# Four convolution layers in one kernel: where the next image's products are asked for, and how layer 3 is entered

## The chip, the cores and the metric

One NeuronCore of a Trainium2 chip runs the whole network in a single launch. The metric is the device time of that launch in microseconds, from the first to the last instruction. Five engines work side by side, each with its own instruction stream: TensorE (PE; its weight loads are shown as PEld), VectorE (DVE), ScalarE (ACT), GpSimd (POOL) and SyncE (SP), which here issues nearly all DMA transfers.

## The reference

The input has 4 images of 256 channels and 48 x 48 pixels. Four layers follow each other, each as `x = x + layer(group_norm(x))`, in float32:

```python
# layer 0: 49 attention weights a pixel, from a 7x7 convolution with dilation 2
k = relu(conv(x, w1, 7x7, dilation 2) + b1)            # 128 channels
k = relu(batch_norm(conv(k, w2, 1x1) + b2))            # 49 channels
attn = softmax(k, axis=1)
out = sum over the 49 taps p of: shifted(x, p) * attn[:, p]
# layer 1: 3x3 convolution of the signs of x with the signs of the weights
# layer 2: 3x3 convolution with ternary weights and a scale for each output channel
# layer 3: linear attention over windows of three sizes
q, k = sigmoid(Wq x), sigmoid(Wk x);  v = Wv x, normalised for each head
for each window: attn = (q . sum over the window of k v) / (q . sum over the window of k)
out = Wout concat(the three) + bout
```

The group norm needs the mean and variance of whole groups of channels over an image. So each layer of an image begins with a chain of small steps (statistics, a matmul that averages over groups, a reciprocal root), and nothing of that layer can start ahead of it.

## The kernel before

Layers 0 to 2 run image by image; layer 3 follows for all images. While image b is in its attention of layer 0, in layer 1 and in layer 2, the 7x7 convolution of image b + 1 is the filler: a generator whose products are asked for in small chunks where TensorE would otherwise wait. A call of `fill(us)` asks for about that much of it.

```python
def fill(us):
    next(side, None)
    owed += us
    while owed > 0:
        n = next(filler, None)          # the next chunk: up to three products of 0.52 nominal us each
        if n is None: owed = 0.0; return
        owed -= n
```

`conv0(b, extra)` is that convolution, in a form with fewer products: for seven points, one after the other, VectorE makes combinations of rows (`v`) and columns (`vx`) of the padded image, TensorE multiplies them by prepared weights (`cv<-vx,wt`), and VectorE gathers the outcome in `y` and `k`. It is 260 products an image. A point's own preparation is spread over the chunks of an earlier point: 8 operations with point 0, 18 each with points 2 and 4, 4 each with points 1, 3 and 5.

```python
class Stats:
    def end(self, wait):
        ... bn_aggr ...
        wait(1.5)                       # a chunk of the filler
        pe.matmul(ps, gmat, mv[:, :, 0]) ; ... ; dve.tensor_add(v, v, mv[:, :, 1])
        wait(2.5)
        pe.matmul(ps, gmat, v) ; ... rsqrt ...

def transpose_x(pad, k):
    for h in range(NPH // 2):
        tr = ps_tr.tile(...)            # one buffer
        ... four transpositions on TensorE ...
        act.copy(xT[...], tr)
        fill(0.7)

def attend(b):                          # layer 0 of image b, from k1 on
    for k in range(NBLK):               # NBLK = 5
        lg = logits(k1, k)              # lg<-w_sb,k
        e = softmax_begin(lg, k)
        ...
        if k < 2: xTs[k] = transpose_x(pad, k); fill(2.6)
        else: fill(4)
    ...                                 # fill(10), then apply0 for each block
```

Layer 2 works on an image in three thirds of 16 rows. For each third, `normalised(h)` normalises the rows, `combine(ts, at)` makes for each of four combinations of rows a high part (VectorE, then a cast on ScalarE) and a low part (a subtraction on GpSimd); TensorE then makes four tiles (`at`) for each of two output halves (`mo`), and `give` adds each to x on VectorE.

```python
def layer2(b, stats):
    m, r = stats.end(fill)
    ...
    ts = normalised(0)
    for at in range(N2):
        combine(ts, at)
        fill(2 if at == 0 else 1)
    for h in range(thirds):
        if b == B - 1 and h == 0:
            proj["first"][0].enough = True
        for mo in range(NCT):
            for at in range(N2):
                if b == B - 1: fill(1.2)
                ps = ps_cv.tile(...)    # two buffers
                ... 12 matmuls: cv<-v,wl ...
                if late: late()         # give of the tile before
                late = functools.partial(give, ps, h, mo, at)
                if mo == NCT - 1 and h < thirds - 1:
                    if at == 0: ts = normalised(h + 1)
                    combine(ts, at)
    if b + 2 < B: fetch_x(b + 2, 0)
    fill(2)
    late()
    m3, r3 = stats.end(fill)            # for layer 3
```

`prelude(b)` is the start of image b: its statistics, the padded copy, the first rows and columns of its convolution. It runs between layer 2 of image b - 2 and the attention of image b - 1, and uses up what is left of the filler.

```python
def prelude(b):
    ...; fill(7)
    for ct in range(NCT):
        for s in range(NRB): stats.take(xts[b], ct, s)     # 6 each
        fill(2)
    m, r = stats.end(fill)
    ... pad ...
    fill(3)
    while stage < len(POINTS) - 1: fill(1)
    for _ in rows_at(pad, (0.0, None)): fill(0.9)
    for _ in columns_at(0.0, XPOINTS[:2]): fill(1)
    fill_all()
    for _ in columns_at(0.0, XPOINTS[2:]): pass

for b in range(B):
    filler = conv0(b + 1, {}) if b + 1 < B else project_first()   # and here, for the last image: the masks
    stats = attend(b)
    ...
    layer2(b, layer1(b, stats))
    if b + 2 < B: prelude(b + 2)
    else: fill_all()
```

For the last image the filler is `project_first`: the projections (q, k, v) of image 0 for layer 3, in twelve groups. When layer 2 of the last image begins, the groups whose rows are not yet asked for are given up (`enough`) and are made inside layer 3. Layer 3 (`s<-qs,ks`, masked copies `sm`, then `acc<-sm,vs`) begins when q, k and v of its first block have been written and read back.

Of the kernel before, what the change touches and what calls it, by code (L numbers as in the profile page):

```python
# [13 lines left out]
BF16 = mybir.dt.bfloat16  # L14
# [7 lines left out]
P = 128  # L22
# [42 lines left out]
N2 = 4  # L65
# [80 lines left out]
def conv_preact_kernel(  # L146
# [101 lines left out]
    def start(job):  # L248
        active.append([step + 1, job])
# [37 lines left out]
    class Projection:  # L287


        def __init__(self, b, scr, psum, tag, shape):  # L290
            self.b, self.scr = b, scr
            self.psum, self.tag, self.shape = psum, tag, shape
            self.xn, self.uses, self.vs = {}, {}, {}

            self.enough, self.left = False, []

        def ps_tile(self):
            t = self.psum.tile(self.shape, F32, tag=self.tag, name="proj_ps")
            return t if len(self.shape) == 2 else t[:, 0]
# [1 line left out]
        def load(self, g, a, n):  # L301

            b = self.b
            yield from take("xr")
            if self.enough:
                free["xr"] += 1
                self.left.append(g)
                return
            xr = self.scr.tile([P, NCT, RB, W], F32, tag="xr", name="xr")
            sync.dma_start(  # L310
                out=xr,
                in_=x3_d[b][:, a * RB : (a + 1) * RB, :].rearrange(
                    "(ct p) r w -> p ct r w", p=P
                ),
            )
            yield FETCH
            yield from take("xn")
            xn = self.scr.tile([P, NCT, NKC, P], F32, tag="xn", name="xn")
            for ct in range(NCT):
                dve.tensor_scalar(  # L320
                    xn[:, ct].rearrange("p c (r x) -> p c r x", x=KC),
                    xr[:, ct].rearrange("p r (c x) -> p c r x", x=KC),
                    st3[:, b, 0, ct : ct + 1],
                    st3[:, b, 1, ct : ct + 1],
                    ALU.subtract,
                    ALU.mult,
                )
                yield 1
            free["xr"] += 1
            self.xn[g], self.uses[g] = xn, n  # L330
# [7 lines left out]
        def qk(self, g, a, name, mo):  # L338
            b = self.b
            while g not in self.xn:  # L340
                if g in self.left:
                    return
                yield 1
            yield from take("kt")
            yield from bank(1)
            ps = self.ps_tile()[:, 0:NB]
            for ct in range(NCT):
                pe.matmul(
                    ps,
                    proj[name][:, ct, mo * P : (mo + 1) * P],  # L350
                    self.xn[g][:, ct],
                    start=(ct == 0),
                    stop=(ct == NCT - 1),
                )
            self.used(g)
            yield 1
            t = self.scr.tile([P, NB], F32, tag="sg", name="sg")
            rows = t.rearrange("p (r c x) -> p c r x", c=NKC, x=KC)
            act.activation(
                rows, ps.rearrange("p (c r x) -> p c r x", c=NKC, x=KC), AF.Sigmoid  # L360
            )
            chans, cols = slice(mo * P, (mo + 1) * P), slice(a * NB, (a + 1) * NB)
            if name == "k":
                kt = self.scr.tile([P, NB], F32, tag="kt", name="kt")
                act.copy(kt.rearrange("p (c r x) -> p c r x", c=NKC, x=KC), rows)
            yield 1
            if name == "k":
                sync.dma_start(out=k_d[b][chans, cols], in_=kt)
            sync.dma_start(out=(q_d if name == "q" else kf_d)[b][chans, cols], in_=t)
            free["kt"] += 1  # L370
            made.add((name, b, mo, a))

        def v(self, g, a, c):
            b = self.b
            while g not in self.xn or (c > 0 and g not in self.vs):
                if g in self.left:
                    return
                yield 1
            if c == 0:
                yield from take("vt")  # L380
# [72 lines left out]
    with (  # L453
# [563 lines left out]
        def transpose_x(pad, k):  # L1017
# [4 lines left out]
            for h in range(NPH // 2):  # L1022
# [6 lines left out]
                            ident,  # L1029
                        )  # L1030
                act.copy(xT[:q, 2 * h : 2 * h + 2, :], tr)
                fill(0.7)
            return xT

        def apply0(xt, k, rows_at_hand, load_next, xTs):
# [46 lines left out]
        def attend(b):  # L1082

            k1, pad, xt = k1s.pop(b), pads[b], xts[b]
            begun = None
            xTs = {}
            for k in range(NBLK):
                lg = logits(k1, k)
                e = softmax_begin(lg, k)
# [54 lines left out]

        def layer1(b, stats):
            xt = xts[b]
            m, _ = stats.end(fill)
            neg = small.tile([P, NCT], F32, tag="neg", name="neg")
            dve.tensor_scalar_mul(neg, m, -1.0)
# [45 lines left out]
        def layer2(b, stats):  # L1195
# [68 lines left out]
                fill(2 if at == 0 else 1)  # L1264
            late = None
            for h in range(thirds):
                if b == B - 1 and h == 0:
                    proj["first"][0].enough = True
                for mo in range(NCT):
                    for at in range(N2):  # L1270
                        if b == B - 1:
                            fill(1.2)
                        ps = ps_cv.tile([P, R2, W], F32, tag="cv3", name="cv3")
                        n = 0
                        for ct in range(NCT):
# [11 lines left out]
                            late()  # L1287
                        late = functools.partial(give, ps, h, mo, at)

                        if mo == NCT - 1 and h < thirds - 1:  # L1290
                            if at == 0:
                                ts = normalised(h + 1)
                            combine(ts, at)
            if b + 2 < B:
                fetch_x(b + 2, 0)
            fill(2)
            late()
            m3, r3 = stats.end(fill)
            dve.tensor_copy(st3[:, b, 0, :], m3)
            dve.tensor_copy(st3[:, b, 1, :], r3)  # L1300

        def prelude(b):
# [6 lines left out]
            for ct in range(NCT):  # L1309
                for s in range(NRB):  # L1310
                    stats.take(xts[b], ct, s)
                fill(2)
            m, r = stats.end(fill)
            off0 = small.tile([P, 1], F32, tag="off0", name="off0")
            dve.scalar_tensor_tensor(off0, m[:, 1:2], -1.0, r[:, 1:2], ALU.mult, ALU.mult)
# [84 lines left out]
        with (  # L1400
# [13 lines left out]
            def project_first():  # L1414
# [7 lines left out]
                    sync.dma_start(out=proj[name], in_=src.rearrange("(ct p) o -> p ct o", p=P))  # L1422
                groups = [(a, ("k0", "v", "q0")) for a in range(NRB)]
                groups += [(a, ("k1", "q1")) for a in range(NRB)]
                proj["first"] = Projection(0, scr, ps, "ps", [P, 512]), groups
                start(paced(proj["first"][0].groups(groups), 1))
                while active:
                    advance()
                    yield 1.2
# [1 line left out]
            for b in range(B):  # L1431
                if b + 1 < B:
                    filler = conv0(b + 1, {})
                else:
                    ending.close()
                    wts3 = ctx.enter_context(tc.tile_pool(name="wts_qkv", bufs=1, side="right"))
                    filler = project_first()
                    masks = wts3.tile([P, NMASK], BF16, name="masks")
                    nc.gpsimd.dma_start(out=masks, in_=masks_in[:, 0:NMASK])
                stats = attend(b)  # L1440
                for _ in side:
                    fill(1)
# [11 lines left out]
    with (  # L1454
# [11 lines left out]
        nc.scalar.dma_start(out=wout_sb, in_=wout.rearrange("(kt p) o -> p kt o", p=P))  # L1466
        bout_sb = wts.tile([P, NCT], F32, name="bout_sb")
        nc.scalar.dma_start(out=bout_sb, in_=bout.rearrange("(ct p) -> p ct", p=P))
        mask = [
            masks[:, MASK_AT[i] : MASK_AT[i] + MROWS[i] * MCOLS[i]].rearrange(  # L1470
                "p (r c) -> p r c", c=MCOLS[i]
# [411 lines left out]
        order = [(b, ct, rb) for b in range(B) for ct in range(NCT) for rb in range(NRB)]  # L1883
        bank_m = ps_m, "st", [P, 512]


        made_first, groups = proj["first"]
        left = [groups[g] for g in made_first.left]
        if left:
            start(paced(Projection(0, scr, *bank_m).groups(left), 1))  # L1890
        for mo in range(NCT):
            start(in_turn([k_sums(b, a, mo) for b in range(B) for a in range(NRB)]))
        start(in_turn(norms(b, rb) for b in range(B) for rb in range(NRB)))

        seen_first = HALVES[0] // RB + 1
        until(("q", 0, 0, 0), *((what, 0, *at) for a in range(seen_first) for what, at in (("k", (0, a)), ("v", (a,)))))
        qs = {0: load_q(*order[0])}
        for a in range(seen_first):
            load_kv(0, 0, a)


        LOADS = {2: (0,), 3: (1, 2), 4: (3, 4), 5: (5,)}
# [120 lines left out]
```

## Time and profile before

The median of three runs is 3850.24 us (3838.81 to 3850.6). The profiled execution has a span of 3848.8 us and a mean granted TensorE clock of 0.943.

| stretch, us from the start | what runs there | PE busy, us | DVE busy, us | PE clock |
|---|---|---|---|---|
| 0 to 254.4 | image 0 and 1 begin, weights of layer 0 are prepared | 144.4 | 209.9 | |
| 254.4 to 455.5 | attention of image 0, weights of layers 1 and 2 | 152.2 | 91.8 | 0.80 |
| 455.5 to 563.2 | layers 1 and 2, image 0 | 101.2 | 68.5 | |
| 752.1 to 863.2 | layers 1 and 2, image 1 | 103.5 | 71.3 | |
| 863.2 to 945.5 | passage from image 1 to 2 | 68.6 | 68.2 | 0.95 |
| 945.5 to 1059.3 | attention of image 2 | 100.7 | 62.4 | 0.93 |
| 1059.3 to 1167.4 | layers 1 and 2, image 2 | 101.1 | 69.7 | |
| 1167.4 to 1237.0 | passage to image 3 | 65.5 | 41.8 | 1.00 |
| 1354.1 to 1480.0 | layers 1 and 2, image 3 | 110.4 | 76.6 | |
| 1480.0 to 1495.0 | entry to layer 3 | 4.4 | 6.7 | 0.59 |
| 1495.0 to 3848.8 | layer 3 | 2093.0 | 1543.0 | 0.97 |

A busy time close to the stretch's length says that the engine sets the pace there. The rest of the stretch is idle time, and the list of waits says what ended it. The granted clock is a share of full speed: at a lower one the same matmul takes longer, and that counts as busy. All operations go through one helper that keeps them in program order, so nearly every line of the profile has the same line number, and the groups are told apart by their tiles.

### The profile page before, as it was taken

What the parts mean: (1) busy time and instruction counts of PE and PEld (TensorE: products, weight loads), DVE (VectorE), ACT (ScalarE), POOL (GpSimd) and SP (SyncE); (2) the same over time, 40 slices, a digit from 0 to 9 for tenths busy, and PEclk for the clock granted to TensorE, in tenths of its full rate; (3) what the DMA queues carried; (4) which work ended last, traced back from release to release, by engine and by line L of the source; (5) the groups of instructions that cost most, each with busy time, mean ns of one, the idle gap of its engine ahead of it and who ended that gap; (6) DMA issues with size and microseconds to landing.
All of it is one profiled execution on the core that took longest, in us unless ns stands there. A gap on an engine that the chain in (4) does not pass through costs nothing. (4 is left out here: it accounts for less than half of the span.)

```text
span 3848.8 us, 68938 instructions
## 1 busy us (share of the span) xinstructions
PE 3300.0 (86%) x26534; PEld 1903.3 (49%) x26534; DVE 2483.7 (65%) x5119; ACT 1028.5 (27%) x2019; POOL 1511.4 (39%) x2183
## 2 busy tenths in 40 slices
PE   3678798998899788898789888899899899988998
PEld 2456676776777655443334333344444344443443
DVE  7873477567565356777656577765577856656655
ACT  0012111211110332443222333332243322233321
POOL 0000030020020023678764576765356856344432
PEclk9788799999999798999899999999999999999999
DMA  7734323413413332345443353434222434101122
GB/s 246 238 117 136 103 85 96 130 65 116 142 45 118 110 105 93 110 144 166 122 135 106 92 152 107 151 100 126 77 95 92 151 107 133 49 30 42 51 58 59
DMA packets 373018, 423.03 MB, mean 110 GB/s; under 512 B 129075, under 2 KB 328531, under 8 KB 371539
## 3 DMA queue, kind: packets, MB, share of 16 engines
q1 hardware_dynamic: 371491, 416.32, 35.0%
q8 instruction: 211, 3.46, 0.4%
q0 software_dynamic: 144, 1.52, 0.2%
q14 instruction: 116, 0.95, 0.1%
q10 hardware_dynamic: 1056, 0.79, 0.1%
HBM read 288.79 MB, written 131.25 MB: 109 GB/s over the span
## 5 line engine op out<-in xcount | busy, mean ns | idle before, releaser
L142 DVE TENSOR_TENSOR sm<-s,masks 128x112 f32<-128x112 f32 (+10 forms) x2592 | 1135.1, 492 | 785.0 <-PE s L142 329.9
L142 POOL TENSOR_TENSOR sm<-sm,masks 128x432 f32<-128x432 f32 (+14 forms) x1152 | 853.5, 754 | 956.9 <-ACT sm L142 705.1
L142 PE MATMUL s<-qs,ks 32*128 32x320 f32 (+3 forms) x5760 | 835.2, 503 | 197.6 <-DVE sm L142 147.3
L142 ACT COPY sm<-s 128x528 f32<-128x528 f32 (+2 forms) x1152 | 594.1, 534 | 1483.4 <-PE s L142 1195.6
L142 PE MATMUL acc<-sm,vs 128*32 128x384 f32 (+18 forms) x13440 | 879.2, 385 | 14.9 <-POOL sm L142 14.6
L142 PEld LDWEIGHTS s<-qs,ks 32*128 32x128 f32 x5760 | 375.6, 187 | 606.1 <-DVE sm L142 234.1
L142 PE MATMUL cv<-vx,wt 128*128 128x288 f32 x2080 | 572.6, 433 | 87.6 <-DVE vx L142 62.0
L142 PEld LDWEIGHTS acc<-sm,vs 128*32 128x32 f32 x13440 | 354.7, 110 | 552.6 <-issue 350.2
L142 PEld LDWEIGHTS cv<-vx,wt 128*128 128x128 f32 x2080 | 413.8, 203 | 212.4 <-issue 57.7
L142 POOL MEMSET v<- 128x16 f32 (+1 forms) x120 | 17.5, 206 | 844.0 <-DVE vx L142 550.4
L142 PE MATMUL cv<-v,wl 128*128 128x384 f32 x1152 | 227.5, 356 | 24.0 <-DVE x L142 16.7
L142 PEld LDWEIGHTS cv<-v,wl 128*128 128x128 f32 x1152 | 213.2, 194 | 36.6 <-DVE x L142 15.7
L142 POOL TENSOR_TENSOR pt<-pt 128x144 f32<-128x144 f32 x336 | 186.9, 556 | 22.7 <-DVE pt L142 0.5
L142 POOL TENSOR_TENSOR v<-l2v,v 128x384 fp32r<-128x384 f32 x96 | 104.4, 1116 | 130.6 <-ACT v L142 130.6
L142 POOL TENSOR_TENSOR nhi<-nhi,nq 128x384 f32<-128x384 f32 x144 | 147.8, 1053 | 0.0
L142 PE MATMUL cv<-pad,wl 128*128 128x384 bf16 x864 | 143.1, 327 | 1.1 <-ACT pad L142 1.1
L142 PE MATMUL out_ps<-o,wout_sb 128*128 128x384 f32 x288 | 122.8, 509 | 9.2 <-DMA rc<-r_d 5.2
L142 ACT ACTIVATE y<-cv 128x288 f32<-128x288 f32 x56 | 20.8, 430 | 376.9 <-PE cv L142 361.5
L142 DVE SCALAR_TENSOR_TENSOR x<-cv,alpha,x 128x384 f32<-128x384 f32 x144 | 83.9, 610 | 57.2 <-PE cv L142 56.8
L142 PE MATMUL out_ps<-stage,wout_sb 128*128 128x384 f32 x288 | 117.6, 490 | 0.4 <-DVE stage L142 0.4
L142 DVE TENSOR_TENSOR x<-x,ap 128x240 f32<-128x240 f32 (+1 forms) x80 | 26.9, 391 | 140.2 <-PE ap L142 139.9
L142 DVE TENSOR_TENSOR vx<-v 128x868 f32<-128x868 f32 x112 | 115.3, 1058 | 0.4
(158 smaller groups left out, 3026.5 us busy)
## 6 DMA issues: line engine op xcount, KB each, us to landing
wt<-wt SPq DMA_DIRECT2D x48, 768.0 KB
kb_d<-pt SPq DMA_DIRECT2D x48, 576.0 KB
rc<-r_d SPq DMA_DIRECT2D x192, 144.0 KB
nhi<-kb_d SPq DMA_DIRECT2D x120, 192.0 KB
nlo<-kb_d SPq DMA_DIRECT2D x88, 192.0 KB
o_d<-stage SPq DMA_DIRECT2D x24, 576.0 KB
o<-o_d SPq DMA_DIRECT2D x24, 576.0 KB
wl<-wl_d SPq DMA_DIRECT2D x16, 768.0 KB
```

The lines of the kernel that those rows point to most:

```text
L142: return lambda *args, **kwargs: self.tc.keep_in_program_order(op(*args, **kwargs))
```

## The change

The change has two sides. In layers 0 to 2 it moves the places where chunks of the next image's convolution are asked for: at the attention's start (`fill(5)`), after each half of a transposition (1.5 in place of 0.7), ahead of each chain of statistics, and among the statistics of the image after next. It also normalises layer 2's next third during the first output half and not the second. On the other side it takes out what the kernel before had at the passage to layer 3: all projections of image 0 are made before layer 3 again, none is made between the tiles of layer 2, the masks are loaded when layer 3 is entered, and k and v of the first block are loaded ahead of q.

```diff
 # Projection: `enough` and `left` are gone
-            if self.enough:
-                free["xr"] += 1
-                self.left.append(g)
-                return
 # transpose_x
-                fill(0.7)
+                fill(1.5)
 # attend, ahead of the first logits
+            fill(5)
 # layer1
+            fill(1.5)
             m, _ = stats.end(fill)
 # layer2
-                if b == B - 1 and h == 0:
-                    proj["first"][0].enough = True
                 for mo in range(NCT):
                     for at in range(N2):
-                        if b == B - 1:
-                            fill(1.2)
...
-                        if mo == NCT - 1 and h < thirds - 1:
-                            if at == 0:
+                        if h < thirds - 1:
+                            if mo == NCT - 1:
+                                combine(ts, at)
+                            elif at == N2 - 2:
                                 ts = normalised(h + 1)
-                            combine(ts, at)
             fill(2)
             late()
+            fill(1.5)
             m3, r3 = stats.end(fill)
 # prelude
                 for s in range(NRB):
                     stats.take(xts[b], ct, s)
-                fill(2)
+                    if s % 2 == 1:
+                        fill(1.2)
+            fill(1.5)
             m, r = stats.end(fill)
 # the masks: from the last image's start to layer 3's start
-                    masks = wts3.tile([P, NMASK], BF16, name="masks")
-                    nc.gpsimd.dma_start(out=masks, in_=masks_in[:, 0:NMASK])
...
+        masks = wts.tile([P, NMASK], BF16, name="masks")
+        nc.gpsimd.dma_start(out=masks, in_=masks_in[:, 0:NMASK])
 # layer 3
-        left = [groups[g] for g in made_first.left]
-        if left:
-            start(paced(Projection(0, scr, *bank_m).groups(left), 1))
...
-        qs = {0: load_q(*order[0])}
         for a in range(seen_first):
             load_kv(0, 0, a)
+        qs = {0: load_q(*order[0])}
```

## The prediction

> **What bounds the kernel now.** I read the page's first two parts first, then the busy time by stretch, then TensorE's waits, then TensorE's timeline from image to image.
>
> ```profile
> PE 3300.0 (86%) x26534; PEld 1903.3 (49%) x26534; DVE 2483.7 (65%) x5119; ACT 1028.5 (27%) x2019; POOL 1511.4 (39%) x2183
> PE   3678798998899788898789888899899899988998
> PEclk9788799999999798999899999999999999999999
> ```
>
> TensorE is the bound, but not evenly: its tenths and its clock dip in the first fifteen slices, layers 0 to 2. Layer 3 begins near 1484 us and holds nothing that the change is aimed at. Busy time by stretch (stretch; its length, then PE, PEld, DVE, ACT and POOL busy; clock; DMA share; GB/s):
>
> ```profile
> 563.20:639.90 76.70, 64.34 (x250) 48.78 (x248) 64.97 (x113) 6.24 (x12) 2.44 (x6) 0.93 0.37 123
> 639.90:752.10 112.20, 100.04 (x556) 81.91 (x557) 61.53 (x135) 23.29 (x49) 2.78 (x10) 0.92 0.40 124
> 1237.00:1354.10 117.10, 90.70 (x449) 71.22 (x450) 47.52 (x140) 48.10 (x88) 8.46 (x16) 0.75 0.44 130
> ```
>
> The first is a passage between images: TensorE misses 12.4 us of 76.7, and VectorE is as busy as TensorE. The second is the attention of layer 0, image 1; the third the same for image 3, where projections of layer 3 are the filler and the clock is only 0.75. TensorE's waits from 254 to 1237 us (sum, times, longest):
>
> ```profile
> PE lg L142 <- ACT k L142: 20.9, 4, 5.6
> PE gn_ps L142 <- DVE gn_mv L142: 14.3, 4, 7.4
> PE trx L142 <- ACT xT L142: 14.3, 7, 6.9
> PE cv L142 <- DVE x L142: 13.6, 19, 4.0
> ```
>
> These four are what the change goes for: the last Relu ahead of an attention, statistics, the two halves of a transposition through one PSUM buffer, and layer 2's accumulations waiting for VectorE. The timeline shows that a wait costs more than its length:
>
> ```profile
> 594.78 39.52 PE L142 MATMUL cv<-vx,wt 128*128 128x288 f32 x160
> 639.89 2.64 PE L142 MATMUL lg<-w_sb,k 128*120 128x49 f32 x8 [5.59 <-ACT k L142]
> 642.33 1.07 PE L142 MATMUL trx<-ident,pad 128*120 128x128 f32 x4
> 643.19 3.09 PE L142 MATMUL cv<-vx,wt 128*128 128x288 f32 x6
> ...
> 649.67 0.94 PE L142 MATMUL lg<-w_sb,k 128*120 128x49 f32 x8
> ```
>
> A product is two records, so 80 of them take 39.52 us: 0.495 us each. After the wait the same eight lg records take 2.64 us and not 0.94, and three products 3.09 and not 1.62.
>
> **What the Trainium skill says.** "TensorE: Matmul & The Clock Gate", in "Why this matters for your kernels", asks for no idle gap over about 3 us between bursts, or the clock halves. The trace agrees for the 5.59 us wait, and shows the same after shorter ones: after 2.35 us near 653 us, 6 products took 4.29 us and not 3.09. "PSUM — Partial Sum Buffer", section "Engine vs sequencer instructions", calls the queues of ScalarE, VectorE and GpSimdE strict first-in-first-out. The trace fits: in image 3 the combined rows of layer 2 stand behind projection work on their engines (part 6). "Perfetto Trace Analysis", "Optimization Strategy", advises interleaving regimes with different bounds, which is the change's method. "DMA: Bandwidth & Descriptors", "Issuing engines are not separate DMA queues", says that transfers from any engine share the same DMA engines; this bears on the masks, whose one load took 14.0 us.
>
> **The change, part by part.** The products of the next image's layer 0 are a fixed supply, 260 an image; nothing is added. I counted in the built order of both kernels how many stand ahead of each point. For images 1, 2 and 3, 140, 127 and 127 precede the previous image's layer 2 before, and 167, 155 and 155 after; 9 of each now stand even ahead of the previous image's first logits.
>
> 1. Relu wait. Nine products, 4.5 us, enter the gap of 5.6 us for three images. They are saved where they stood, and most of the slow clock goes too: 1.7 (lg) + 0.5 (trx, 1.07 for 0.60) + 1.5 (products) = 3.7, of which I count 3. Gain 3 x 7.5 = 22.5 us.
> 2. Statistics of the image after next. Waits of 4.42 us (near 590) and 7.40 us (near 888) get nine more products each: 4.4 + 4.5, and 2 us of slow clock each (12 records took 5.15 us after the second, 3.17 elsewhere). Gain 12.9. The wait of 9.87 us near 200 I count as nothing: from 49 to 254 us VectorE is busy 177 of 205 us.
> 3. Given back. With fewer products left in the passage, VectorE becomes its bound. From layer 2's end to the next softmax its list after is 22 row combinations x 0.93, 8 vx x 1.03, 12 statistics x 0.55, 12 k x 0.69, 8 y x 0.42, 2 pad x 0.87 and 1.9 of small ones: 50.6 us, and some 3 us of waits, against 89 products x 0.495 = 44 and the 1 us left of the Relu gap. That is 8.5 us lost; for the next image (54.3 us of VectorE, 99 products) 7. Loss 15.5.
> 4. Transpositions. Waits for xT are 14.3 + 2.6 us over three images; one, 6.9 us, is ScalarE held up by something else, where one chunk fits. I take 10 us, and 1.7 us of slow clock twice: 13.
> 5. Thirds of layer 2. Beside the second output half VectorE now has, per third, 4.75 us of results (six x 0.61 and two statistics in each half), 8 x 0.8 combining and 2.0 normalising, 13.2 us, against four tiles of 2.46 = 9.8: hence waits of 0.5, 0.9 and 0.2 us at each third, 3.2 an image. With the normalising in the first half it has 11.2, and one tile of slack in PSUM. I leave 0.6 an image: gain 2.6 x 4, say 10. Two smaller waits of image 0, 2.3 us after layer 2 and some 2 of 3.3 at its start, go as well: 4.3. For images 1 and 2 the start stays: the heavier row work now falls between its statistics and its normalising.
> 6. Image 3. Projection matmuls move from layer 2 (10 to 0) and from layer 3 (8 to 0) into the attention (48 to 64). From the second statistics matmul (1397.5) to layer 2's first tile (1415.4) it takes 18 us, in image 2 4.4; after, no v group but the last stands there, so I expect 10: gain 8. Layer 2 loses 10 x 0.49 = 5, the attention gains 16 x 0.49 = 8, half in gaps: net 9. Layer 3 gets rid of 8: gain 3.
> 7. Start of layer 3. q is now loaded after eight loads of k and v, each issued about 0.5 us after the other from 1481. But before, too, the second scores waited 6.42 us for k until 1492. Loss 2. The masks are now asked for behind GpSimd's last subtraction of layer 2 (1466): 14 us bring them by 1480, before the first use at 1486.
>
> Sum: 22.5 + 12.9 - 15.5 + 13 + 10 + 4.3 + 9 + 3 - 2 = 57. I take 50 of it, since parts 1 to 4 need every chunk's data in time: 3850 - 50 = **3800 us**.
>
> **The rivals.** First, VectorE takes over all of it: it is 85% busy in the passage, and the first row combinations of the image after next now stand ahead of the softmax. For it speaks 64.97 against 64.34; against it that the moved work goes to the attention, where VectorE has 61.5 of 112 us. Then parts 1 to 3 come to nothing and the time is near 3830. Second, the passage to layer 3 was the larger thing: masks and q late, nothing overlapped. Against it speaks the order of the loads; if it holds, the masks cost up to 14 us and the time is 3815. Third, the clock matters more than I count: image 3's attention at 0.75 rising to 0.9 would give some 14 us more (90.7 x (1 - 0.75/0.9) = 15), and 3770 to 3785 come within reach.
>
> **Range and chances.** From 3770 (rival three, and part 3 small) to 3832 (rival one). 2% under 3850 is 3773, at the edge: 0.10 for faster by over 2%, 0.89 within, 0.01 slower.
>
> **What would show it.** Right, if the wait of lg for k falls from 5.6 to about 1 us in three images; if statistics wait under 2 us; if TensorE's waits for x inside layer 2 nearly vanish; if VectorE fills over 90% of the passage from layer 2 to the next logits, which shrinks from 76.7 to some 62 us; if layer 3 takes as long as before within 5 us. Wrong, if the passage stays near 76 us, if image 3's attention grows by over 8 us, or if layer 3's first scores stand more than 5 us later behind layer 2's last tile.

## The result and the profile after

The kernel after takes 3798.97 us, the median of four runs (3788.04 to 3809.47), against 3850.42 for the kernel before on the same chip: a ratio of 0.9873, 95% interval 0.9839 to 0.9907. The prediction was 3800. The total held, but errors in opposite directions stand behind it, as the stretches show. The starts of the stretches are read off TensorE's timeline in each profile (the first scores `lg` of an attention, the first product of layer 1 and of layer 2, and so on), and the lengths are in us.

| stretch | before | after | difference |
|---|---|---|---|
| start, to the first scores | 254.5 | 252.3 | -2.2 |
| attention of image 0 | 201.0 | 190.5 | -10.5 |
| three passages (after images 0, 1, 2) | 76.7, 82.3, 69.6 | 57.2, 65.0, 56.1 | -50.3 |
| attention of images 1, 2 | 112.2, 113.8 | 110.0, 112.6 | -3.4 |
| layer 1 to layer 2, images 0, 1, 2 | 45.1, 46.1, 45.0 | 46.1, 48.9, 48.9 | +7.7 |
| layer 2, images 0, 1, 2 | 62.6, 65.0, 63.1 | 64.8, 60.1, 63.5 | -2.3 |
| attention of image 3 | 117.1 | 141.0 | +23.9 |
| layer 1 to layer 2, image 3 | 61.4 | 57.9 | -3.5 |
| layer 2, image 3, to the end of its last tile | 64.6 | 54.1 | -10.5 |
| entry to layer 3, to its first sums `acc` | 16.9 | 22.9 | +6.0 |
| the rest of layer 3 | 2351.9 | 2343.2 | -8.7 |

Images 0 to 2 with the start give 61 us; image 3, the entry and layer 3 together take back 7.

The page of after shows the same instructions on TensorE and VectorE, and five more on ScalarE (2024 against 2019). TensorE's busy time is 28 us less for the same 26534 records, at a mean granted clock of 0.951 for 0.943.

```profile
PE 3272.3 (86%) x26534; PEld 1886.4 (50%) x26534; DVE 2487.1 (66%) x5119; ACT 1034.1 (27%) x2024; POOL 1512.9 (40%) x2183
PE   3678898998997787988889789899999899989998
PEclk9798899999998898999999899999999999999999
```

Busy time by stretch of after, with the columns of the prediction's (stretch; its length, then PE, PEld, DVE, ACT and POOL busy; clock; DMA share; GB/s): the first passage, the attention of image 1, the attention of image 3.

```profile
553.70:610.90 57.20, 53.07 (x214) 40.23 (x213) 53.09 (x98) 7.79 (x13) 2.95 (x8) 0.97 0.43 147
610.90:720.90 110.00, 101.45 (x599) 84.07 (x598) 66.21 (x142) 23.32 (x50) 2.67 (x10) 1.00 0.45 138
1175.90:1317.00 141.10, 101.07 (x485) 75.94 (x486) 56.33 (x161) 65.20 (x111) 11.61 (x22) 0.79 0.41 130
```

In the passage TensorE now misses 4.1 us of 57.2 and not 12.4 of 76.7, and it has 36 records fewer: 11.3 us of the 19.5 are busy time that went elsewhere or ran faster, 8.2 are idle time. Those 36 belong to image 1 and went ahead: image 0's attention holds 802 records for 769. The second line shows the same move one image on: image 1's attention holds 43 records more, with 37 fewer in the passage behind it (239 for 276), and is still 2.2 us shorter, at a clock of 1.00 for 0.92. So the work moved into gaps that were there, and the gaps' slow clock went too. In the third line, image 3, 36 records more cost 24 us. TensorE is idle for 40 us there, and the clock is 0.79.

TensorE's waits from 252 to 1176 us (sum, times, longest), the kinds that the change went for:

```profile
PE cv L142 <- DVE x L142: 12.3, 9, 6.1
PE trx L142 <- ACT xT L142: 12.3, 6, 4.6
PE lg L142 <- ACT k L142: 5.2, 5, 4.2
PE gn_ps L142 <- DVE gn_mv L142: 3.8, 3, 3.4
```

Scores waited 20.9 us for the last Relu and wait 5.2 now; the 4.2 us of image 3 are in both sums. Statistics went from 14.3 to 3.8. The other two kinds hardly fell, though the timeline shows that one of them changed its place:

```profile
501.83 15.80 PE L142 MATMUL cv<-v,wl 128*128 128x384 f32 x72 [6.08 <-DVE x L142]
517.88 18.02 PE L142 MATMUL cv<-v,wl 128*128 128x384 f32 x96 [0.25 <-DVE x L142]
```

From one third of layer 2 to the next the wait is 0.25 us now (0.5, 0.9 and 0.2 before), but at layer 2's start TensorE waits 6.08 us (3.26 before, for ScalarE). VectorE's timeline says why. The lines below stand between the statistics at layer 1's end (479.88 us) and the first results of layer 2 that VectorE adds to x (501.08), beside layer 2's own normalising and combining; a row combination of the next image (`v`, `va`) takes some 0.9 us. The new places had carried the next image's chunks to a point that needs several of these, and in the kernel before none of them stood here (two column combinations `vx` did):

```profile
480.06 0.87 DVE L142 SCALAR_TENSOR_TENSOR va<-va,v 128x744 f32<-128x744 f32 x1
...
482.32 1.90 DVE L142 SCALAR_TENSOR_TENSOR v<-va,v 128x744 f32<-128x744 f32 x2
484.13 0.93 DVE L142 SCALAR_TENSOR_TENSOR v<-pad 128x744 f32<-128x744 f32 x1
...
488.62 0.92 DVE L142 SCALAR_TENSOR_TENSOR va<-pad 128x744 f32<-128x744 f32 x1
...
492.04 1.68 DVE L142 SCALAR_TENSOR_TENSOR v<-pad 128x744 f32<-128x744 f32 x1
```

At the end of the passage after image 0 TensorE no longer waits for Relu, but for VectorE, which is busy 53.09 of its 57.2 us, and the scores then run at full speed (eight records in 0.94 us, 2.64 before):

```profile
604.75 6.34 PE L142 MATMUL cv<-vx,wt 128*128 128x288 f32 x18 [2.87 <-DVE y L142]
610.92 0.94 PE L142 MATMUL lg<-w_sb,k 128*120 128x49 f32 x8
```

At the entry to layer 3 the first scores stand 14 us behind the end of layer 2's last tile, waiting for the reading back of q. Before, they stood 4 us behind it, and the second scores then waited 6.42 us for k. First after, then before:

```profile
1443.27 1.66 PE L142 MATMUL s<-qs,ks 32*128 32x384 f32 x8 [10.30 <-DMA qs<-q_d]
```

```profile
1483.99 1.66 PE L142 MATMUL s<-qs,ks 32*128 32x384 f32 x8
1492.08 1.77 PE L142 MATMUL s<-qs,ks 32*128 32x384 f32 x8 [6.42 <-DMA ks<-k_d]
```

### The profile page after: what moved, and what is told of

Read it like the earlier page. It is cut to its first block, busy times and chain, and to the rows that moved or that the text cites. A ratio compares the mean times of both kernels' runs of the same rounds, so it can differ in the third digit from the quotient of the medians.

```text
span 3795.1 us, 68918 instructions
## 1 busy us (share of the span) xinstructions
PE 3272.3 (86%) x26534; PEld 1886.4 (50%) x26534; DVE 2487.1 (66%) x5119; ACT 1034.1 (27%) x2024; POOL 1512.9 (40%) x2183
## 5 line engine op out<-in xcount | busy, mean ns | idle before, releaser
L142 PE MATMUL acc<-sm,vs 128*32 128x384 f32 (+18 forms) x13440 | 878.7, 385 | 12.9 <-POOL sm L142 12.7
L142 PE MATMUL cv<-vx,wt 128*128 128x288 f32 x2080 | 563.7, 427 | 90.4 <-DVE vx L142 50.3
L142 PEld LDWEIGHTS cv<-vx,wt 128*128 128x128 f32 x2080 | 405.5, 199 | 212.5 <-issue 50.7
L142 PE MATMUL out_ps<-o,wout_sb 128*128 128x384 f32 x288 | 122.6, 508 | 10.5 <-DVE o L142 6.5
L142 POOL TENSOR_TENSOR sq<-vt 128x256 f32<-128x256 f32 x72 | 48.8, 680 | 201.9 <-ACT vt L142 171.7
L142 PEld LDWEIGHTS <-wl 128*128 128x128 bf16 x864 | 83.8, 97 | 59.1 <-issue 0.2
```

The lines of the kernel that those rows point to most:

```text
L142: return lambda *args, **kwargs: self.tc.keep_in_program_order(op(*args, **kwargs))
```

## The experiments

The expectations call theories by letters: A says that the side of layers 0 to 2 brings the gain, B that the passage side does; C and D are two readings of image 3's attention, which e_last_old was to part; E is the version that keeps both sides but image 3's old places; F says that ScalarE's table loads set the pace of image 3's attention; G says that the stores of finished projections do. Times are medians, beside runs of the kernel before on the same chip; ratios are to the kernel before, with 95% intervals. Where two variants are compared, their medians may be from different chips; the medians of the kernel before on these chips lie between 3850.07 and 3851.93 us. Lengths of stretches come from one profile each. Where several profiles have the same order of instructions in a stretch, they show its scatter: the three passages together take 228 to 229 us in three profiles with before's order and 176 to 179 in six with after's, so they are steady; the attention of image 3 takes 108.8 to 117.1 us in six profiles with before's order, of which the kernel before itself is the longest, and 141.0 and 146.4 in two with after's.

### The two sides apart

**e_neither** is the kernel after with its side of layers 0 to 2 undone, so that it has neither side.

```diff
 # after -> e_neither
-                fill(1.5)                  # transpose_x
+                fill(0.7)
-            fill(5)                        # ahead of the first scores
-            fill(1.5)                      # layer1; also layer2's end
 # thirds normalised in the second output half again
 # prelude: fill(2) per half of the statistics again
```

> The kernel after with all of layers 0 to 2 put back (old places of the chunks, thirds normalised late): neither side of the change. Theory A, the passage to layer 3 was worth next to nothing and the chunks and thirds bring it all: 3850 to 3860 us, and the kernel after is some 55 us below this. Theory B, the passage was worth much and the change gave that up: 3870 us or more.

Measured: 3862.74 us, ratio 1.0027 (1.0014 to 1.0039). So the side of layers 0 to 2, on its own, is worth 64 us (3862.74 to 3798.97), and the passage side, which the change took out, was worth 12 us (3862.74 against 3850.59; 5 to 15 by the interval). The time lies between the ranges of A and B, nearer to A's. That 12 is a difference of larger numbers: without it, layer 2's last tile to the first sums takes 50.5 us and not 16.9, but layer 2 of image 3 takes 58.8 and not 64.6, and the rest of layer 3 takes 2339.4 and not 2351.9.

**e_both** is the kernel before with the new places and the early thirds, and the passage side kept.

```diff
 # before -> e_both: every "+" of the change in layers 0 to 2, nothing of the rest
```

> The kernel before with the new places of the chunks and the earlier thirds, and with its passage to layer 3 kept: both sides. Theory A: 3790 to 3800 us, like the kernel after. Theory B: 3780 us or less. The trace of the kernel after has the first scores of layer 3 14 us behind the last tile of layer 2, the one before 4 us, so the entry alone should give 5 us or so.

Measured: 3801.36 us, ratio 0.9869 (0.9846 to 0.9892), the same as after within the intervals. With the new places the passage side adds nothing in sum: they draw the projections forward themselves, and what the earlier entry saves (from layer 2's last tile to the first sums 15.9 us for 22.9) is paid for in image 3, whose attention takes 151.9 us, 11 more than in after. A stands and B falls.

**e_thirds** is the kernel before with only layer 2's thirds normalised in the first output half.

```diff
 # before -> e_thirds
-                        if mo == NCT - 1 and h < thirds - 1:
-                            if at == 0:
+                        if h < thirds - 1:
+                            if mo == NCT - 1:
+                                combine(ts, at)
+                            elif at == N2 - 2:
                                 ts = normalised(h + 1)
-                            combine(ts, at)
```

> The kernel before with the thirds of layer 2 normalised sooner and nothing else. By the prediction 10 us less, 3840 us, and TensorE's waits for x at the thirds of layer 2 down from 3.2 us an image to under 1. Rival: the earlier normalising pushes a give back and the wait only moves: 3848 to 3852 us.

Measured: 3837.08 us, ratio 0.9964 (0.9947 to 0.998), a gain of 13.5 us. Layer 2 shrinks by 3.2, 3.3, 2.0 and 3.0 us in the four images, 11.5 in all, and TensorE's waits for x up to image 3's first scores fall from 13.6 to 5.5 us.

**e_last_old** is the kernel after with image 3's attention at its old places.

```diff
 # after -> e_last_old
-            fill(5)
+            if b < B - 1:
+                fill(5)
-                fill(1.5)                  # transpose_x
+                fill(more)                 # 1.5, and 0.7 for the last image
```

> The kernel after, but in the attention of image 3 the chunks are asked for as before (0.7 at a transposition, nothing ahead of the first logits). Theory C, each projection chunk costs some 2.4 us wherever it stands in layers 0 to 2 and only moves: the attention of image 3 falls from 141 to about 120 us, layer 2 and its end grow by as much, and the time stays at 3795 to 3803 us. Theory D, the chunks stand in bad places there: 3775 to 3785 us.

Measured: 3810.0 us, ratio 0.9891 (0.9864 to 0.9919), 11 us slower than after. The attention of image 3 falls from 141.0 to 125.9 us, but the projections that it no longer holds come at the worst place, behind layer 2, where nothing lies beside them. C and D both fall. Nor are these all the old places: the chunk ahead of layer 1's statistics, `fill(1.5)`, stays in image 3 and falls into its attention's stretch, which holds 108 records of projections (104 before, 140 in after). Stretch from layer 2's last tile to the first scores, in e_last_old; TensorE is busy 17.78 us of 44.10:

```profile
1417.20:1461.30 44.10, 17.78 (x45) 9.54 (x44) 12.46 (x35) 12.09 (x20) 3.80 (x14) 0.68 0.67 193
```

### Image 3, and VectorE's list in the passages

**e_best** keeps both sides and gives image 3's attention its old places, in the hope of its shorter attention without the drain.

```diff
 # e_both -> e_best: the edit of e_last_old
```

> Both sides, but in the attention of image 3 the chunks stand as in the kernel before. Theory E, new places pay in images 0 to 2 and cost in image 3, and the old passage pays only with them there: image 3 starts at 1175 us as in the kernel after, takes the 247 to 260 us to layer 3's first sums that it takes in the kernel before and in the one with the thirds alone (276 in the kernel after), layer 3 follows in 2353: 3775 to 3790 us. Theory A, sides and places just add (3801 with both, 11 more for old places in image 3 as in the last run): 3805 to 3815 us.

Measured: 3795.82 us, ratio 0.986 (0.9835 to 0.9884). From image 3's first scores to layer 3's first sums it takes 260.7 us and not 276.0, at the upper end of what was expected, but the rest of layer 3 takes 2354.0 and not 2343.2. This stretch scatters, yet all profiles agree: in the seven whose layer 3 still makes the groups that are left over (520 records of projections) it takes 2344 to 2356 us, 2351 on average, in the seven others (504 records) 2335 to 2348, 2342 on average. So 16 records more cost some 10 us there, far more than their matmul time. The total lies between the ranges of E and A; over after no gain is shown, since the intervals overlap. Over e_last_old, which differs only by the passage side, it is 14 us faster by the medians (the intervals overlap): with fewer projections in image 3's attention that side seems to pay.

**e_exp** takes ScalarE's table switches away as a suspect. In image 0's projections for layer 3 it computes Exp where the kernel has Sigmoid, so its result is not the reference's; the function's time is the same (490 and 492 ns), but it shares a table with the softmax.

```diff
 # after -> e_exp
-                    rows, ps.rearrange("p (c r x) -> p c r x", c=NKC, x=KC), AF.Sigmoid
+                    rows, ps.rearrange(...), AF.Exp if self.tag == "ps" else AF.Sigmoid
```

> The kernel after with Exp in place of Sigmoid in the projections ahead of layer 3 (image 0 of layer 3 is then something else; all else stays): 6 fewer loads of function tables in image 3. Theory F, ScalarE's chain of table loads sets the pace of the attention of image 3: it shrinks by 8 us or more (6 x 1.28) from 141 us, and the time falls to 3785 to 3792 us. Theory G, the stores of q, k and v and their buffers set it: within 3 us of 141, 3796 to 3802 us.

Measured: 3792.06 us, ratio 0.9847 (0.9832 to 0.9862). Groups of ScalarE in image 3's attention (count; busy time and mean ns; idle time ahead and what ended it), first e_exp, then after, then before:

```profile
L142 ACT ACT_TABLE_LOAD x13 | 16.7, 1283 | 4.4 <-DMA kf_d<-sg 3.4 <-DMA q_d<-sg 0.8
L142 ACT ACTIVATE sg<-proj_ps 128x384 f32<-128x384 f32 x16 | 7.8, 490 | 9.8 <-PE proj_ps L142 6.2 <-DMA q_d<-sg 3.7
```

```profile
L142 ACT ACT_TABLE_LOAD x19 | 24.4, 1283 | 4.6 <-DMA kf_d<-sg 3.4 <-DMA q_d<-sg 0.8
```

```profile
L142 ACT ACT_TABLE_LOAD x13 | 16.7, 1283 | 0.6 <-PE proj_ps L142 0.4
```

Six loads of 1.28 us are gone, 7.7 us, and the attention goes from 141.0 to 138.1 only, as G had it: part of the time that ScalarE won turned into longer waits for the stores (19.0 us in all, 15.9 in after; of these `sg` behind the store of q 3.7, 2.2 in after). The time, 3792.06, lies at the upper edge of F's range and below G's, and its interval overlaps that of after, so it decides nothing. So F accounts for some 3 us of the 24, and even these are within the scatter (146.4 us in e_pad_after). "ScalarE: Activation LUTs", "What ACT_TABLE_LOAD costs", of the Trainium skill gives about 1283 ns for the load, and the trace has exactly that; the further drain of about 1380 ns that it adds is not seen here. ScalarE's timeline in after (start, us, instruction) has a load directly behind one activation and directly ahead of the next:

```profile
1204.07 0.49 ACT L142 ACTIVATE sg<-proj_ps 128x384 f32<-128x384 f32 x1 [2.24 <-DMA q_d<-sg]
1204.57 1.28 ACT L142 ACT_TABLE_LOAD   x1
1205.87 0.22 ACT L142 ACTIVATE vs<-ss 128x24 f32<-128x24 f32 x1
```

**e_pad_after** and **e_pad_before** repeat the writing of image 2's and image 3's padded copy four times in all, which changes no result and adds six VectorE instructions of 0.87 us, 5.2 us, to two passages of each kernel.

```diff
+            for py in list(range(DIL)) * (3 if b >= 2 else 0):
+                dve.tensor_scalar(pad[:, 0, ...], by_phase(xts[b][0])[:, py], m[:, 0:1], r[:, 0:1], ...)
```

> The kernel after with VectorE's two writes of the padded copy made four times in the passages to images 2 and 3 (the same values again): 5.2 us more of VectorE's work in each of two passages. If VectorE bounds the passage now, as the prediction has it: 8 to 11 us more in all, each passage 4 to 5.5 us longer. Rival, TensorE still bounds it (its busy time there is 53.1 of 57.2 us, as VectorE's): under 4 us in all.

> The kernel before with the same 5.2 us more of VectorE's work in each of two passages. There VectorE waited 9.5 us for products in the first passage, so the prediction's view has it absorbed: 0 to 3 us more in all. If VectorE bounds the passage in both kernels: 8 to 11 us more.

Measured: 3810.2 us (ratio 0.9895, 0.9871 to 0.992) for after and 3858.86 us (1.0016, 1.0004 to 1.0028) for before. The two passages grow by 4.7 and 2.8 us in after, by 2.5 and 6.6 in before; the medians grow by 11 and 7 us, so the totals hold scatter from other stretches too. The first passage of e_pad_after, then of e_pad_before:

```profile
556.50:618.40 61.90, 54.98 (x213) 41.17 (x212) 57.81 (x103) 7.81 (x13) 2.95 (x8) 0.94 0.41 136
```

```profile
563.50:642.70 79.20, 64.43 (x250) 48.55 (x248) 69.73 (x119) 6.29 (x12) 2.44 (x6) 0.92 0.36 119
```

That after does not absorb VectorE's work was expected, though its second passage grew by less than the 4 us forecast (VectorE is busy 57.45 of 65.0 us there). That before absorbs so little of it, 1.3 of 10.4 us in sum, was not: VectorE's list lies on the path in both kernels, although TensorE idles 12 us in the first passage before. That idle time stands in two spots, ahead of the statistics and ahead of the scores (6.8 and 5.6 us). The first is a wait for statistics that VectorE makes, the second for the Relu of rows `k` that VectorE finishes last, so it was no slack for more work in VectorE's list.

### The parts of the side of layers 0 to 2, each alone

**e_relu** is before with one filler ahead of the first scores of images 0 to 2, **e_stats** before with the filler at the statistics, **e_trx** before with more of it at the transpositions of images 0 to 2.

```diff
 # before -> e_relu
+            if b < B - 1:
+                fill(5)
 # before -> e_stats
+            fill(1.5)                      # layer1; also layer2's end
-                fill(2)                    # prelude
+                    if s % 2 == 1:
+                        fill(1.2)
+            fill(1.5)
 # before -> e_trx
-                fill(0.7)
+                fill(more)                 # 1.5, and 0.7 for the last image
```

> The kernel before, with one addition: ahead of the first scores of attention in images 0 to 2 chunks of the next image's layer 0 are asked for, so that TensorE has work while the Relu rows are made (the first part of the prediction). Prediction's reading: the wait of 5.6 to 7.5 us ahead of the first scores goes in three images, 15 to 22 us in all, time 3828 to 3836. Rival (TensorE only catches up with VectorE, whose list in the passage stays as long): the wait turns into waits for VectorE at the chunks themselves, under 8 us gained, 3843 to 3851. If the changed places act only together, this alone gives less than a third of the 60 us that the side of layers 0 to 2 is worth.

> The kernel before, with one addition: chunks of the next image's layer 0 are asked for where TensorE waits for statistics (ahead of attention's normalisation, at layer 1 and at the end of layer 2). Prediction's reading: 13 us of waits less, time 3835 to 3842. Rival: the chunks would have stood in the passage anyway and their VectorE work is only moved, under 4 us, 3846 to 3851. For image 3 the same places take projections of layer 3, so layer 2's end may shift there by some us either way.

> The kernel before, with one addition: chunks are asked for at the transpositions of attention's input in images 0 to 2, where TensorE waits for ScalarE's copies. Prediction's reading: 13 us less, 3834 to 3841. Rival: the waits for the copies are replaced by waits for VectorE's rows in the chunks, under 4 us, 3846 to 3851. With the early thirds (13 us measured) and the two runs beside this one, the four parts add to about 60 us if they act independently; a sum below 40 means that they act through each other.

Measured: e_relu 3825.87 us, ratio 0.9936 (0.9915 to 0.9957); e_stats 3857.22, 1.002 (1.0007 to 1.0033); e_trx 3849.8, 0.9996 (0.9981 to 1.0011). So -24, +7 and 0 us; with -13.5 of e_thirds some -31. The four edits together are exactly e_best, and that is worth -56. The parts act through each other, and the table shows where (differences to before, us; e_stats's profile was itself 16 us slower than its median, so its row is read with care):

| | three passages | attention 0 | attention 1, 2 | layer 1 to 2, images 0 to 2 |
|---|---|---|---|---|
| e_relu | -11.4 | -13.9 | +9.8 | -0.3 |
| e_stats | -8.3 | +8.7 | +8.8 | 0.0 |
| e_trx | -26.8 | +20.4 | +3.6 | +12.7 |
| e_thirds | -0.3 | +0.1 | +1.3 | 0.0 |
| e_best, all four | -50.3 | -7.2 | -3.4 | +7.7 |
| after | -50.3 | -10.5 | -3.4 | +7.7 |

In the passages the parts add: 11.4 + 8.3 + 26.8 + 0.3 = 46.8, against 50.3. But e_stats and e_trx alone pay for that in the attentions, by 17.5 and 24.0 us. (In e_stats image 3 pays as well: its attention takes 130.8 us, where the new chunk ahead of layer 1 brings 4 records of projections more.) The waits show one way in which the parts meet. Up to image 3's first scores TensorE's waits for xT are 14.3 us in before; with chunks ahead of the first scores alone (e_relu) they grow to 22.4, with more chunks at the transpositions alone (e_trx) they fall to 7.2, and in after they are 12.3. Attention of image 0 in e_trx:

```profile
253.10:474.50 221.40, 175.05 (x799) 146.21 (x800) 94.23 (x187) 43.10 (x77) 3.32 (x13) 0.75 0.37 114
```

There it ran 30 records more than before (799 against 769), worth 6 us at before's rate in this stretch (152.11 / 769 = 0.198), and yet TensorE's busy time is 23 us more, at a clock of 0.75 (0.80 before, 0.86 after). The rest goes with the clock. In the same stretch the weights of layers 1 and 2 are prepared, and TensorE's waits for them depend on where chunks are left to fill in, before and then after:

```profile
PE sum_ps L142 <- DVE wl L142: 21.7, 5, 10.9
```

```profile
PE sum_ps L142 <- DVE wl L142: 10.3, 2, 6.1
```

This kind is 6.8 us in e_relu, 16.9 in e_trx and 25.3 in e_stats. So an item of 11 us, the largest of TensorE's waits in the window that the prediction listed and not among its four lines, is part of the change's gain in images 0 to 2; in e_relu its 14.9 us less are as much as the whole gain of this stretch, 13.9. Why the clock of this stretch differs so much from one arrangement to another these runs do not settle. Only a part of it belongs to the arrangement: it is 0.80 in before and 0.75 in e_neither, which has before's order here, and 0.86 in after and 0.81 in e_bufs below, which has after's.

### Why image 3's attention grew

**e_bufs** is the kernel after with more buffers for what the projections store.

```diff
 # after -> e_bufs, for image 0's projections ahead of layer 3
-            t = self.scr.tile([P, NB], F32, tag="sg", name="sg")
+            t = self.scr.tile([P, NB], F32, tag="sg", name="sg", bufs=4 ...)   # 2 before
 # the same for kt, 2 -> 4, and vt, 1 -> 2
```

> The kernel after, with more buffers for what the projections ahead of layer 3 store (values one to two, gates and keys two to four). Theory G: ScalarE waits in image 3's attention for the stores of earlier projections (9.5 + 3.4 + 2.2 + 0.8 us), and this is most of the 24 us by which that attention grew: attention of image 3 falls from 141 to 125 to 130 us, time 3783 to 3792. Rival: the pace is set by ScalarE's own work and by the two result banks, so attention stays within 4 us of 141 and time at 3795 to 3803.

Measured: 3785.68 us, ratio 0.9821 (0.9797 to 0.9844); the attention of image 3 takes 119.7 us, 21.3 less than in after. ScalarE's waits in that stretch, first before, then after, then e_bufs:

```profile
ACT vt L142 <- DMA v_d<-vt: 8.2, 2, 7.3
...
ACT sg L142 <- DMA q_d<-sg: 2.2, 1, 2.2
```

```profile
ACT vt L142 <- DMA v_d<-vt: 9.5, 4, 3.7
...
ACT L142 <- DMA kf_d<-sg: 3.4, 1, 3.4
...
ACT sg L142 <- DMA q_d<-sg: 2.2, 1, 2.2
```

```profile
ACT seen L142 <- PE tra L142: 16.0, 18, 2.2
ACT e L142 <- DVE e L142: 12.3, 5, 5.2
...
ACT vt L142 <- PE proj_ps L142: 5.9, 5, 2.8
```

The waits for stores are gone from e_bufs's whole list. TensorE's waits for ScalarE's gates fall with them, in part. Before, after and then e_bufs:

```profile
PE proj_ps L142 <- ACT sg L142: 5.4, 4, 2.8
```

```profile
PE proj_ps L142 <- ACT sg L142: 17.9, 6, 3.9
```

```profile
PE proj_ps L142 <- ACT sg L142: 11.9, 4, 3.3
```

And the whole stretch in e_bufs, beside that of after above:

```profile
1186.20:1305.90 119.70, 89.02 (x485) 67.70 (x486) 56.62 (x161) 64.96 (x111) 12.31 (x22) 0.90 0.49 153
```

The same 485 records, the same 19 table loads, 9.3 us less idle time on TensorE and 12.1 us less busy time at a clock of 0.90 for 0.79. G stands as to after, and the rival within 4 us falls: waiting for buffers that were still being stored cost that attention 21.3 us, more than twice the scatter seen. How much of the growth of 24 us this is stays open. The kernel before waited for stores too, 10.4 us of ScalarE's time against 15.9, and might also gain from more buffers; no run shows it. And TensorE's waits for gates are still 11.9 us in e_bufs, against 5.4 before. What is shown is that with more buffers the 36 records more cost 2.6 us over the kernel before (119.7 for 117.1), or 11 over the shortest profile with its order. The saving in the whole time, 13 us, is smaller than the 25 us from image 3's first scores to layer 3's first sums (251.0 against 276.0): in the profile, images 0 to 2 took 10 us more, most of it at the lower clock in image 0's attention, and the rest of layer 3 took 4 more. At 0.9821, e_bufs beats the kernel before clearly. Its interval just touches that of after (0.9839 to 0.9907); the stretch shows the mechanism more surely than the totals do.

## Why the prediction was right, and where it was not

The time was right because an error in images 0 to 2 (45 us expected of the parts there, 61 measured with the start) and one in image 3 and the entry (10 us of gain expected there, thirds aside, 7 of loss measured with all) cancelled, and because 7 us had been left off the sum. That the errors were of like size was luck.

- **Part 1, the Relu wait.** Right in its mechanism: the waits went from 5.6 to under 1 us in three images, and the slow scores after them with them. Alone it gave 24 us, where 22.5 were counted, but that agreement is partly luck: the passages gave 11.4 of it, image 0's attention gave 13.9, with 14.9 us less of waits for weights, and the other two attentions took back 9.8.
- **Part 2, statistics.** The waits fell by 10.5 us; the two that the prediction named held 11.8, and with their slow clock it counted 12.9. But alone these places made the kernel 7 us slower, in part through image 3, where they draw projections: a wait that goes is not yet time that is saved.
- **Part 3, VectorE becomes the bound.** Right for the first passage: 53.09 of 57.2 us is 93%, and 5.2 us more of VectorE's work lengthened it by 4.7. In the second, 88% busy, the same work added 2.8, and in the third TensorE is the bound (51.98 of 56.1 us, VectorE 30.71). Wrong in what it takes as its start: VectorE's list was on the path before too, by e_pad_before. The passages shrank to 57.2, 65.0 and 56.1, further than the 62 that the prediction gave for the first; its own list of VectorE's work, 50.6 us and some 3 of waits, came nearer.
- **Part 4, transpositions.** The waits for xT hardly fell, from 14.3 to 12.3 us, because, by the single runs, the chunks of part 1 lengthen them and these shorten them again. What these places bring is seen in the passages, 26.8 us alone, because the supply of chunks is fixed and each that runs early is missing later. The prediction booked the gain in the wrong stretch. How much of the surplus of 16 us in images 0 to 2 is theirs, how much lies in the 11.4 us fewer of waits for weights in image 0, and how much is the clock's, stays open.
- **Part 5, thirds.** Right: 11.5 us of layer 2 alone, where 10 were counted. The start of layer 2 was wrong: in image 0 its wait grew from 3.26 to 6.08 us, and the stretches from layer 1 to layer 2 took back 7.7 us, 6.7 of them in images 1 and 2, where the prediction had the start stay as it was. By the table the places at the transpositions bring this (12.7 us in e_trx alone). So TensorE's waits for x did not vanish: those between thirds did, and this one came.
- **Part 6, image 3: the step that failed.** "the attention gains 16 x 0.49 = 8, half in gaps": it grew by 24 us. Layer 2 lost 10.5 us, 3.0 of them by the thirds (e_thirds), and not 5, the stretch from layer 1 to layer 2 lost 3.5 and not 8. The step priced the moved projections by TensorE's matmul time. e_bufs shows a term that was missing: each projection has to leave through a buffer that is free only when its store has landed, and with one buffer for v and two for gates and keys this held up ScalarE, then TensorE, and the clock was lower with it. With more buffers the stretch took 21.3 us less, though part of that may be time that the kernel before lost as well.
- **Part 7, entry to layer 3.** Loss 6.0 and not 2: the first scores waited 10.30 us for q. Layer 3 itself gained 8.7 and not 3, outside the 5 us allowed; the leftover groups cost about 10 us there, by the averages under e_best, and not their matmuls.
- **The rivals.** VectorE took not all of it; the passage to layer 3 was not the larger thing (e_both equals after). Of the third rival there is something: the mean clock rose from 0.943 to 0.951, though in image 3's attention, where it was expected, only from 0.75 to 0.79.

Of the three signs that were to make the prediction wrong, two came true, image 3's growth and the late first scores; the total was right all the same.

## What to carry to other kernels

Price moved work by everything that it needs on its way out, the buffer and its store first, and not by its engine time; where work from a second source is pulled into a stretch, look at what the copying engine waits for. Filler from a fixed supply gains nothing by the wait that it fills, but by what it no longer does later, so look for the gain in the stretch where the supply used to be used up. Try places together as well as alone: here they gave -24, +7, 0 and -13 us alone and -56 together. And before calling a stretch's growth the work of one cause, see what the kernel before already lost to it.

## What was not expected of the hardware

The granted clock goes with most of the scatter from run to run. Over 32 runs of the kernel before, from 3836.26 to 3863.22 us at clocks from 0.939 to 0.947, time and clock have a correlation of -0.89, and a straight line gives 31 us for 0.01 of clock. A profile is one such run, so one stretch can be some us off with the same instructions: 117.1, 108.8 and 110.1 us for image 3's attention in before, e_thirds and e_pad_before, at clocks of 0.75, 0.81 and 0.82.

With more buffers for a store the clock was higher: in image 3's attention 0.90 for 0.79 (0.77 in e_pad_after, with after's order), which goes with over half of the gain there (12.1 of 21.3 us). "Perfetto Trace Analysis", "Optimization Strategy", says that the same gap repeating can mean too few buffers for the next tile. Here ScalarE's gaps of up to 3.7 us behind stores had that cause, since they are gone in e_bufs; of TensorE's gaps behind ScalarE's gates, up to 3.9 us long, a third went (17.9 to 11.9 us).
